# A twelve-block network: diagonals on TensorE in a state-space scan, a sum scan for a decay, keys projected behind another block, and an attention whose maxima go in threes

## The chip, the cores and the metric

The kernel runs on one core of a Trainium2 chip. The metric is the device time of one execution in microseconds (us), the median of several runs. The engines named below are PE (TensorE, matrix products, with PEld for its weight loads), DVE (VectorE), ACT (ScalarE), POOL (GpSimd) and SP (SyncE, which issues DMA transfers). PE writes its results to PSUM, from where DVE, ACT or POOL take them to SBUF.

## The reference, cut to what matters

`x` is [B=4, T=128, C=128], the context is [4, 2048, 96]. Twelve blocks are applied in turn, each as `x = x + block(layernorm(x))`: a 1-bit attention, a two-way mamba, a feed-forward layer, a 12-head attention over the context, an rwkv layer, a mixture of experts, an 8-head attention over the context, an ALiBi attention, a 1-bit feed-forward layer, a third attention over the context (the fourth layer's), a causal attention and a routed feed-forward layer. Three of them matter in detail:

```python
# mamba, once forward and once on flipped x; 256 channels d, 16 states n
def step(h, inp):
    u_t, d_t, b_t, c_t = inp
    dA = exp(d_t[:, :, None] * A)
    h = h * dA + (d_t * u_t)[:, :, None] * b_t[:, None, :]
    return h, einsum('bdn,bn->bd', h, c_t)
# rwkv: the decay of a step, and the state
w_log = -softplus(-(w0 + tanh(xw @ w1) @ w2)) - 0.5
decay = exp(-exp(w_log))          # = exp(-exp(-0.5) * sigmoid(...))
state = state * d_t + (state @ a_t) b_t + v_t k_t
# fourth layer's context attention: 8 heads of 16, keys and values from the context
q, k, v = x @ Wq + bq, y @ Wk + bk, y @ Wv + bv
out = softmax(q k^T / 4) v        # per head, over 2048 keys
return out @ Wo + bo
```

## The kernel before, in words

Everything is f32 unless said. `x` stays in SBUF as [token, batch, channel]. The blocks are methods of a class `Net` and run one after another (`program`, L2166). The code is written in a tile framework: tiles come from pools with a number of buffers, the framework adds the waits, and it may order the instructions of an engine differently from the text where nothing forbids it. Weights of the next block are fetched by `nxt()`.

Most blocks begin alike: DVE and ACT do the layer norm (`layernorm`, L343; its square root is `ln_sd`, L338, on ACT), PE turns the result over (`transposed`, L394, tiles `tr_...`), and the copy of that is the right side of the first products. While the norm runs, `busy` (L378) issues ten bf16 products on PE whose results nobody uses; they go into the tile that the transposes then overwrite. ACT's functions live in tables: when a function of another table is called, the profile shows an ACT_TABLE_LOAD of 1.28 us ahead of it.

**bit_attention** goes over units; `values` (L1112) of a unit multiplies probabilities with values into `av` and sums them (`rsum`), both from a pool of two PSUM banks (`mm`). The scores use another pool, `stp`.

**mamba** (L1238). `setup(d)` of a direction makes xd (L1285, transposes), the convolution, `xdbl`, `delta` (`softplus`, L1220, table functions Exp and Ln) and `du = delta*u` (L1344). Three bf16 parts of B and C (`x3`) are kept. The loop goes over d = 0, 1 and over n = 0 to 15. For each n, `spread` (L1349) puts row n of B (`b_ps`) and of C (`c_ps`, copied to `cs` by ACT) on all partitions with a small bf16 product; DVE makes `dbu = du*b_ps` (L1364, 128x1024); ACT makes `dA = exp(delta*A)` (L1370), in PSUM, for each half; DVE runs the recurrence for each half (L1373, `tensor_tensor_scan`, 128x512); POOL makes `hc = h*cs` (L1376); PE adds hc into `y_ps` (L1378). `setup(1)` runs in between the n of direction 0.

**grouped_ffn** (L1399): ten warming products, transposes (`tr_xnT`, L391), eight h_ps products with Gelu (L1418, L1419), y_ps products (L1425). The next block is a context attention, whose weights are first folded per group of four heads (`fold`, L473: `a_ps`, `o_ps`), from a PSUM pool of its own. Two folds are placed after h_ps 4 and 7, what is left after the block (`fold_rest`). The folds read `r_qk` and `r_vo`, which arrive by DMA. The moe block does the same for the later context attention, in expert 0 and expert 4.

**rwkv** (L1433): six mixed inputs, products through `mm` (L1457), on ACT in this order Tanh for `lo`, Square, Sigmoid for `dec` (L1502), Exp, Sigmoid for `a`, for `lg`, and Sqrt for `nrm` (L1515). The decay products within a chunk of time come from a multiplying scan `Dp`; `D = dec*Dp` and `Di = 1/D` (L1564, DVE reciprocal, 128x512) scale `al`, `be`, `kh` and `rh`, and the chunk's products follow.

**alibi, bit_ffn, narrow attention.** Behind alibi, `narrow_keys` (L679) fetches the key and value weights `w_kv` on SP and projects keys (`k_ps`, L700, copied to `kT` by ACT) and values (`v_ps`, L711, copied to `v`) of batch elements 0 and 1. Then bit_ffn runs (sums `tot` L2014, `wm`, quantized `q`, `q_tr` L2052, `h_ps` L2058). `narrow_attention` (L717) has heads in two groups s of four; one head takes 32 rows of PE. `maxima(b, s)` makes 16 products `s_ps` (L771: one head by 512 keys), each reduced to its maximum by DVE (`na_m`, L774), three PSUM banks; then `m_tr` turns the maxima over, and they are put into q. `weighted` makes transposed scores `t_ps` (L793, 32 products for four chunks of keys), Exp on ACT (`p`, L799, two of 128x1024), and 32 products into `av` (L806), these one step late. The two are woven by hand: in each of the four steps of a (b, s), two maxima, t_ps, two maxima, av; the maxima are those of the next (b, s). Batch elements 2 and 3 are projected during the steps of b = 1 and 2 with s = 0. `finish` (L816), the end of a batch element, runs in one go within the first step of the next: four copies of 17 rows by ACT and DVE in turn, `o_tr` (L822), reciprocal and multiply, `on_tr`, `oT`, `y`, add to x.

Of the kernel before, what the change touches and what calls it, by code (L numbers as in the profile page):

```python
# [18 lines left out]
P = 128  # L19
# [252 lines left out]
class Net:  # L272
# [60 lines left out]
    def root(self, v, name, eps=0, scale=1.0):  # L333

        nc = self.nc
        n = v.shape[1]
        sd = self.small(n, name + "_sd")
        nc.scalar.activation(sd, v, AF.Sqrt, bias=self.eps[:, eps : eps + 1], scale=scale)  # L338
        r = self.small(n, name + "_r")
        nc.vector.reciprocal(r, sd)  # L340
        return r

# [104 lines left out]
    def fold_open(self, es, n, heads, mask, bo):  # L447
# [11 lines left out]
        ps = raw.enter_context(self.tc.tile_pool(name=f"xr{n}_ps", bufs=2, space=PSUM))  # L459
# [6 lines left out]
        self.folds = [lambda h=h: self.fold(ps, w, h, heads, mask) for h in range(0, heads, 4)]  # L466

    def fold_rest(self):
        while self.folds:
            self.folds.pop(0)()  # L470
        self.raw.close()

    def fold(self, ps, w, h, heads, mask):  # L473
# [10 lines left out]
        mm = ps.tile([P, 512], F32, tag="xw", name="a_ps")  # L484
# [13 lines left out]
        mm = ps.tile([P, 512], F32, tag="xw", name="o_ps")  # L498
# [180 lines left out]
    def narrow_keys(self, es):  # L679

# [4 lines left out]
        self.kvp = es.enter_context(self.tc.tile_pool(name="na_kv", bufs=2))  # L685
        self.kv = {}
        with self.tc.tile_pool(name="na_kvps", bufs=3, space=PSUM) as ps:
            for b in range(2):
                for self.kv[b] in self.project(ps, b, self.nc.scalar.copy):
                    pass  # L690
# [26 lines left out]
    def narrow_attention(self, nxt):  # L717
# [9 lines left out]
        with ExitStack() as es:  # L727
# [4 lines left out]
            sp = es.enter_context(tc.tile_pool(name="na_s", bufs=3, space=PSUM))  # L732
# [3 lines left out]
            self.busy(tr, self.x, 10)  # L736
            self.layernorm(self.x, xn)
            nc.vector.tensor_add(self.x, self.x, bc_mid(self.row("bo3"), B))
# [7 lines left out]
            for s in range(2):  # L746
                nc.tensor.matmul(mm[:, s], wqo[:, s * P : s * P + P], xT, start=True, stop=True)
                nc.vector.tensor_scalar(
# [7 lines left out]
            os = []  # L756
            for j in range(2):
                t = one.tile([P, 2, P], F32, name=f"o{j}")
                nc.gpsimd.memset(t, 0.0)
                os.append(t)  # L760
            nxt()

            def maxima(b, s, kT):
# [3 lines left out]
                for j in range(4):  # L767
                    for g in range(4):
# [4 lines left out]
                        at = j * 4 + g  # L773
                        nc.vector.tensor_reduce(part[:, at : at + 1], t, axis=AX, op=ALU.max, negate=True)  # L774
                        yield
# [40 lines left out]
            def finish(b, av):  # L816
                o = os[b % 2]
                for g in range(0, P, 32):
                    self.copy(o[g : g + VW], av[g : g + VW])
# [7 lines left out]
                nc.vector.tensor_mul(on, heads[:, :, 0:ND], bc_in(r, ND))  # L827
                tr = sp.tile([P, B, P], F32, tag="s", name="on_tr")
                nc.tensor.transpose(tr[:, 0], self.flat(on), self.ident)
                oT = wk.tile([P, P], F32, tag="oT", name="oT")  # L830
                nc.scalar.copy(oT, tr[:, 0])
                y = sp.tile([P, B, P], F32, tag="s", name="y")
                nc.tensor.matmul(y[:, 0], oT, wqo[:, 2 * P : 3 * P], start=True, stop=True)
                nc.vector.tensor_add(self.x[:, b], self.x[:, b], y[:, 0])

            def run(*gens):

                gens = [iter(g) for g in gens if g is not None]
                while gens:
                    gens = [g for g in gens if next(g, gens) is not gens]  # L840
# [8 lines left out]
            take(maxima(0, 0, kv[0]), 17)  # L849
            done = None  # L850
            for b in range(B):
                av = avp.tile([P, 2, P], F32, tag="av", name="av")
                ahead = self.kv.get(b + 1)
                more = iter(()) if ahead or b + 1 == B else iter(self.project(sp, b + 1, nc.scalar.copy))
                for s in range(2):
# [5 lines left out]
                    for i in range(NCH // 4):  # L861
                        take(top, 2)
                        next(steps)
                        ahead = next(more, ahead)
                        take(top, 2)
                        next(steps)
                        if done:
                            finish(*done)
                            done = None
# [1338 lines left out]
```

## Time and profile before

| | |
|---|---|
| median of 4 runs | 1457.83 us (1454.09 to 1459.52) |
| profiled execution: own time, span | 1457.64 us, 1455.4 us |
| mean PE clock granted | 0.896 of full |
| busy: PE, DVE, ACT, POOL | 1174.9, 936.1, 644.6, 160.4 us |
| instructions | 16113 |

The blocks lie in the span about so (us): bit_attention 0 to 180, mamba to 361, grouped_ffn to 396, the 12-head context attention to 762, rwkv to 923, moe to 1004, the 8-head one to 1092, alibi to 1139, narrow_keys to 1172, bit_ffn to 1196, narrow attention to 1400, causal to 1418, routed to 1455.

In the profile's lines, `a<-b` is output and input of an operation by the program's names, L and a number the line in the kernel, x and a number how many there are. Numbers are us, or ns where a group's mean is meant. In timeline lines, what stands in brackets is the engine's idle time before the operation and what ended it. One matrix product in f32 shows as two records on PE.

### The profile page before, as it was taken

What the parts mean: (1) busy time and instruction counts of PE and PEld (TensorE: products, weight loads), DVE (VectorE), ACT (ScalarE), POOL (GpSimd) and SP (SyncE); (2) the same over time, 40 slices, a digit from 0 to 9 for tenths busy, and PEclk for the clock granted to TensorE, in tenths of its full rate; (3) what the DMA queues carried; (4) which work ended last, traced back from release to release, by engine and by line L of the source; (5) the groups of instructions that cost most, each with busy time, mean ns of one, the idle gap of its engine ahead of it and who ended that gap; (6) DMA issues with size and microseconds to landing.
All of it is one profiled execution on the core that took longest, in us unless ns stands there. A gap on an engine that the chain in (4) does not pass through costs nothing.

```text
span 1455.4 us, 16113 instructions
## 1 busy us (share of the span) xinstructions
PE 1174.9 (81%) x6362; PEld 620.9 (43%) x6373; DVE 936.1 (64%) x1632; ACT 644.6 (44%) x865; POOL 160.4 (11%) x153
## 2 busy tenths in 40 slices
PE   2477557676899999999996735899979748999978
PEld 0156322223644444444433314575444434565644
DVE  8987678897257667766765797513667365544635
ACT  3732255443356555655654210233645531444432
POOL 0036105365000000000000120000004000000000
PEclk9788668799999999999999976999999866999989
DMA  6000000000600000000001000510000000000010
GB/s 180 0 1 2 0 1 0 29 1 18 183 0 0 0 0 0 1 0 0 1 0 58 1 0 1 144 27 22 0 2 2 10 6 1 2 2 2 2 55 8
DMA packets 9486, 27.84 MB, mean 19 GB/s; under 512 B 1191, under 2 KB 7120, under 8 KB 8350
## 3 DMA queue, kind: packets, MB, share of 16 engines
q1 hardware_dynamic: 8286, 24.88, 6.0%
q10 hardware_dynamic: 1120, 1.88, 0.4%
q8 instruction: 52, 0.85, 0.2%
q14 instruction: 28, 0.23, 0.0%
HBM read 26.49 MB, written 0.26 MB: 18 GB/s over the span
## 4 chain that ended last, share of the span: by engine, by line
PE 63%; DVE 17%; ACT 5%; issue 4%; POOL 1%; DMA 1%; another core or an unknown queue 0%; DVEq 0%; ACTq 0%; SPq 0%; POOLq 0%
PE av L615 14%; PE sc L581 13%; PE s_ps L771 5%; DVE h L1373 3%; PE t_ps L793 2%; PE k_ps L700 2%; PE h_ps L1801 2%; PE y_ps L1813 2%; PE mm L1457 2%; PE y_ps L1378 2%; PE av L806 1%; POOL hc L1376 1%; PE q_ps L533 1%; DVE dbu L1364 1%; PE v_ps L711 1%
## 5 line engine op out<-in xcount | busy, mean ns | idle before, releaser
L615 PE MATMUL av<-s,ctx 128*97 128x512 f32 x448 | 208.0, 600 | 6.5 <-ACT s L613 6.4
L581 PE MATMUL sc<-q_aug,ctxT 99*128 99x512 f32 x448 | 209.1, 593 | 0.0
L612 DVE TENSOR_TENSOR s<-s,mbs 128x1024 f32<-128x1024 f32 x112 | 132.3, 1217 | 38.8 <-ACT mbs L607 38.8
L583 ACT COPY s<-sc 128x1024 f32<-128x1024 f32 x112 | 113.0, 1009 | 96.6 <-PE sc L581 96.3
L613 ACT ACTIVATE s<-s 128x1024 f32<-128x1024 f32 x112 | 115.4, 1056 | 35.6 <-DVE s L612 35.0
L591 DVE TENSOR_TENSOR m<-m,s 128x1024 f32<-128x1024 f32 x72 | 87.9, 1221 | 65.0 <-ACT s L583 65.0
L774 DVE TENSOR_REDUCE na_m<-s_ps 128x1 f32<-128x512 f32 x128 | 83.0, 686 | 69.4 <-PE s_ps L771 69.1
L615 PEld LDWEIGHTS av<-s,ctx 128*97 128x97 f32 x448 | 73.5, 166 | 125.7 <-issue 105.0
L581 PEld LDWEIGHTS sc<-q_aug,ctxT 99*128 99x128 f32 x448 | 81.0, 189 | 88.0 <-issue 77.8
L1378 PE MATMUL y_ps<-hc,consts 128*128 128x512 f32 x128 | 76.2, 729 | 29.3 <-POOL hc L1376 27.8
L799 ACT ACTIVATE p<-t_ps 128x1024 f32<-128x1024 f32 x64 | 62.4, 1021 | 63.7 <-PE t_ps L793 62.0
L771 PE MATMUL s_ps<-kT,q 32*128 32x512 f32 x256 | 84.5, 710 | 1.7 <-DVE na_m L774 1.7
L1376 POOL TENSOR_TENSOR hc<-h,cs 128x1024 f32<-128x1024 f32 x32 | 75.8, 2380 | 85.6 <-DVE h L1373 85.5
L1373 DVE TENSOR_TENSOR_SCAN h<-dA,dbu 128x512 f32<-128x512 f32 x64 | 74.1, 1201 | 4.1 <-ACT dA L1370 4.0
L1378 PEld LDWEIGHTS y_ps<-hc,consts 128*128 128x128 f32 x128 | 26.4, 226 | 82.4 <-POOL hc L1376 56.5
L793 PE MATMUL t_ps<-q,kT 32*128 32x128 f32 x1024 | 55.6, 297 | 1.6 <-ACT p L799 1.6
L1370 ACT ACTIVATE dA<-delta,A 128x508 f32<-128x508 f32 x64 | 42.8, 687 | 29.4 <-DVE h L1373 29.2
L793 PEld LDWEIGHTS t_ps<-q,kT 32*128 32x128 f32 x1024 | 45.9, 195 | 14.6 <-issue 9.4
L382 PEld LDWEIGHTS <-consts 128*128 128x128 bf16 x169 | 18.7, 120 | 69.3 <-issue 54.9
L1479 POOL TENSOR_SCALAR pick_r<-consts,cols 128x16 f32<-128x16 f32 x1 | 0.5, 484 | 408.2 <-PE av L615 408.2
L1817 DVE SCALAR_TENSOR_TENSOR x<-y_ps,cw,x 128x128 f32<-128x128 f32 x32 | 9.0, 343 | 48.0 <-PE y_ps L1813 44.1
L700 PE MATMUL k_ps<-ctxT,w_kv 97*128 97x512 f32 x64 | 34.6, 685 | 5.8 <-DMA w_kv<-in_kv 5.8
(603 smaller groups left out, 2015.8 us busy)
## 6 DMA issues: line engine op xcount, KB each, us to landing
w_moe<-in_moe SPq DMA_DIRECT2D x2, 2048.0 KB, 8.6
ctxT<-in_ctxT SPq DMA_DIRECT2D x3, 768.0 KB
w_l3f<-in_l3f SPq DMA_DIRECT2D x1, 1920.0 KB, 7.6
rows<-in_rows ACTq DMA_DIRECT2D x1, 1664.0 KB, 12.7
w_l0f<-in_l0f SPq DMA_DIRECT2D x1, 1024.0 KB
w_mamba<-in_mamba SPq DMA_DIRECT2D x1, 976.0 KB, 18.6
w_r<-in_r SPq DMA_DIRECT2D x1, 960.0 KB
consts<-in_consts SPq DMA_DIRECT2D x1, 832.0 KB, 16.8
```

What stands on the lines that cost most here:

```text
L581: nc.tensor.matmul(sc[:, i], self.ctxT[:, at : at + P], u.q, start=True, stop=True)
L583: nc.scalar.copy(s, sc)
L591: nc.vector.tensor_max(u.m, u.m, u.s[j])
L612: nc.vector.tensor_sub(p, p, bc_mid(u.mb, 2))
L613: nc.scalar.activation(p, p, AF.Exp)
L615: nc.tensor.matmul(u.av[: DC + 1], self.ctx[:, u.b * NCH + chunks[2 * j + i]], p[:, i], start=j + i == 0, stop=j == n - 1 and i == 1)
L771: nc.tensor.matmul(t, qs[rows], kT[rows, s, j * 512 : j * 512 + 512], start=True, stop=True)
L774: nc.vector.tensor_reduce(part[:, at : at + 1], t, axis=AX, op=ALU.max, negate=True)
L793: nc.tensor.matmul(ts[g // 2][:, g % 2, j], kT[g * 32 : g * 32 + 32, s, at : at + P], qs[g * 32 : g * 32 + 32], start=True, stop=True)
L1373: nc.vector.tensor_tensor_scan(h[:, half], self.flat(dA), dbu[:, half], 0.0, ALU.mult, ALU.add)
L1376: nc.gpsimd.tensor_mul(hc, h, bc_mid(cs, 2))
L1378: nc.tensor.matmul(y[:, half], self.ident, hc[:, half], start=n == 0, stop=n == 15)
```

## The change

It is one bundle of edits, block by block:

- bit_attention: the last unit's `av` and `rsum` take banks of the scores' pool.
- mamba: ten warming products become seven, and ten each are added before `xdbl` and the first transposes of du; the Ln table is called for ahead of its use; dA moves from PSUM to SBUF; for three of four n, `dbu` is no longer made by DVE but by PE, as du transposed (`duT`) times a diagonal matrix of B's row (`dg`, four ACT activations each), into PSUM (`dbu_ps`, three banks); `hc` has two buffers in place of three.
- folds use the running block's own PSUM tiles; moe's first fold moves behind the block.
- rwkv: the decay is summed by a scan before the exponential, and two Exps give D and Di; the ACT functions are re-ordered so that fewer tables change; six warming products in place of ten in its second half.
- `table` calls for a table ahead of its use (grouped_ffn, moe, narrow attention); `zero_after` makes a zero that depends on a tile, to hold an order.
- narrow_keys runs behind bit_ffn; only the DMA of its weights stays where it was (`narrow_open`).
- narrow attention: maxima in groups of 3, 2, 3, 2, 3, 2, 1, products of a group ahead of its reduces; `finish` in four parts spread over the steps, with one copy in place of four; seven warming products in place of ten; both q products ahead of their DVE work.
- causal and routed: six warming products in place of ten.

```diff
+    def table(self, func, last):
+        self.nc.scalar.activation(self.small(1, "table"), last, func, bias=self.eps[:, 0:1], scale=0.0)
+    def zero_after(self, x, name):
+        z = self.small(1, name)
+        self.nc.vector.tensor_scalar(z, x, 0.0, 0.0, ALU.max, ALU.min)
+        return z
...
-        self.folds = [lambda h=h: self.fold(ps, w, h, heads, mask) for h in range(0, heads, 4)]
-    def fold_rest(self):
+        self.folds = [lambda ps, h=h: self.fold(ps, w, h, heads, mask) for h in range(0, heads, 4)]
+    def fold_rest(self, ps):
         while self.folds:
-            self.folds.pop(0)()
-        self.raw.close()
+            self.folds.pop(0)(ps)
...
-    def narrow_keys(self, es):
+    def narrow_open(self, es):
         pool = es.enter_context(self.tc.tile_pool(name="na_w", bufs=1))
         self.wkv = pool.tile(list(self.A["kv3"].shape), F32, name="w_kv3")
         self.nc.sync.dma_start(self.wkv, self.A["kv3"])
         self.kvp = es.enter_context(self.tc.tile_pool(name="na_kv", bufs=2))
+        self.nps = es.enter_context(self.tc.tile_pool(name="na_s", bufs=3, space=PSUM))
+    def narrow_keys(self):
         self.kv = {}
-        with self.tc.tile_pool(name="na_kvps", bufs=3, space=PSUM) as ps:
-            for b in range(2):
-                for self.kv[b] in self.project(ps, b, self.nc.scalar.copy):
-                    pass
+        for b in range(2):
+            for self.kv[b] in self.project(self.nps, b, self.nc.scalar.copy):
+                pass
...
-            self.busy(tr, self.x, 10)
+            self.busy(tr, self.x, 7)
             self.layernorm(self.x, xn)
+            self.table(AF.Exp, self.sd[:, 0:1])
...
+                at = 0
+                for n in (3, 2, 3, 2, 3, 2, 1):
+                    several = []
+                    for at in range(at, at + n):
+                        j, g = divmod(at, 4)
                         t = sp.tile([P, 512], F32, tag="s", name="s_ps")
                         rows = slice(g * 32, g * 32 + 32)
                         nc.tensor.matmul(
                             t, qs[rows], kT[rows, s, j * 512 : j * 512 + 512], start=True, stop=True)
-                        at = j * 4 + g
+                        several.append((at, t))
+                    for at, t in several:
                         nc.vector.tensor_reduce(part[:, at : at + 1], t, axis=AX, op=ALU.max, negate=True)
-                        yield
+                    at += 1
+                    yield
...
             def finish(b, av):
-                o = os[b % 2]
-                for g in range(0, P, 32):
-                    self.copy(o[g : g + VW], av[g : g + VW])
+                o = wk.tile([P, 2, P], F32, tag="o", name="o")
+                nc.scalar.copy(o, av)
+                yield
                 tr = sp.tile([P, B, P], F32, tag="s", name="o_tr")
                 for s in range(2):
                     nc.tensor.transpose(tr[:, s], o[:, s], self.ident)
@@ -825,20 +839,16 @@
                 nc.vector.reciprocal(r, heads[:, :, ND])
                 on = wk.tile([P, NH, ND], F32, tag="on", name="on")
                 nc.vector.tensor_mul(on, heads[:, :, 0:ND], bc_in(r, ND))
+                yield
                 tr = sp.tile([P, B, P], F32, tag="s", name="on_tr")
                 nc.tensor.transpose(tr[:, 0], self.flat(on), self.ident)
                 oT = wk.tile([P, P], F32, tag="oT", name="oT")
                 nc.scalar.copy(oT, tr[:, 0])
+                yield
                 y = sp.tile([P, B, P], F32, tag="s", name="y")
                 nc.tensor.matmul(y[:, 0], oT, wqo[:, 2 * P : 3 * P], start=True, stop=True)
                 nc.vector.tensor_add(self.x[:, b], self.x[:, b], y[:, 0])
...
-                        take(top, 2)
+                        take(top, 1)
                         next(steps)
+                        take(fin, 1)
                         ahead = next(more, ahead)
-                        take(top, 2)
+                        take(top, 1)
                         next(steps)
                         if done:
-                            finish(*done)
-                            done = None
+                            fin, done = finish(*done), None
+                        take(fin, 1)
                         ahead = next(more, ahead)
                         if s == 0:
...
+                        if u is units[-1]:
+                            return stp.tile([P, W], F32, tag="st", name=name)
+                        return ps.tile([P, 512], F32, tag="mm", name=name)
...
+        if first:
+            self.table(AF.Ln, e[:, 0, 0:1])
...
-                t = das.tile([P, B, T], F32, name=f"dA{j}")
-                nc.vector.memset(t[:, :, 0:1], 0.0)
+                t = one.tile([P, B, T], F32, name=f"dA{j}")
+                nc.gpsimd.memset(t[:, :, 0:1], 0.0)
...
+                duT = wk.tile([P, 2, B, P], F32, tag="duT", name="duT")
+                for half in range(2):
+                    nc.vector.tensor_mul(du[:, half], delta[:, half], u[:, half])
+                    tr = mm_tile("du_tr").rearrange("p (b t) -> p b t", b=B)
+                    if d == 0 and half == 0:
+                        self.busy(tr, e[:, 0].rearrange("p (b t) -> p b t", b=B), 10)
+                    for b in range(B):
+                        nc.tensor.transpose(tr[:, b], du[:, half, b * T : b * T + T], self.ident)
+                    nc.scalar.copy(duT[:, half], tr)
+                yield u, zs, x3, bt, delta, du, duT
...
-                    bn = spread(x3, n, "b_ps")
                     cn = spread(x3, 16 + n, "c_ps")
                     cs = lp.tile([P, N], F32, tag="cs", name="cs")
                     nc.scalar.copy(cs, cn)
-                    dbu = lp.tile([P, 2, N], F32, tag="dbu", name="dbu")
-                    nc.vector.tensor_mul(dbu, du, bc_mid(bn, 2))
+                    if n % 4 == 3:
+                        t = lp.tile([P, 2, N], F32, tag="dbu", name="dbu", bufs=2)
+                        nc.vector.tensor_mul(t, du, bc_mid(spread(x3, n, "b_ps"), 2))
+                        dbu = [t[:, half] for half in range(2)]
+                    else:
+                        dg = lp.tile([P, B, T], F32, tag="dg", name="dg")
+                        for b in range(B):
+                            nc.scalar.activation(dg[:, b], self.ident, AF.Copy, scale=bt[:, b, n : n + 1])
+                        dbu = []
+                        for half in range(2):
+                            t = dps.tile([P, N], F32, tag="dbu", name="dbu_ps")
+                            for b in range(B):
+                                nc.tensor.matmul(
+                                    t[:, b * T : b * T + T], duT[:, half, b], dg[:, b], start=True, stop=True)
+                            dbu.append(t)
...
-                            h[:, half], self.flat(dA), dbu[:, half], 0.0, ALU.mult, ALU.add)
-                    hc = lp.tile([P, 2, N], F32, tag="hc", name="hc")
+                            h[:, half], self.flat(dA), dbu[half], 0.0, ALU.mult, ALU.add)
+                    hc = lp.tile([P, 2, N], F32, tag="hc", name="hc", bufs=2)
...
+            self.table(AF.Sqrt, hT[:, 7, 0:1])
...
+                cum = tmp("cum", pool=ta)
+                nc.vector.tensor_tensor_scan(cum, self.flat(keep), dec, 0.0, ALU.mult, ALU.add)
+                z = self.zero_after(lg[:, 0:1], "rw_z1")
                 nc.vector.tensor_scalar(nkk, k, self.col("k_k"), -1.0, ALU.mult, ALU.mult)
-                nc.vector.tensor_mul(nkk, nkk, self.flat(m))
+                nc.vector.tensor_mul(nkk, nkk, self.flat(rl))
+                nc.scalar.activation(
+                    D[:, :, 1:], cum.rearrange("p (c t) -> p c t", t=CH), AF.Exp, bias=z,
+                    scale=-math.exp(-0.5))
+                nc.scalar.activation(Di, cum, AF.Exp, bias=z, scale=math.exp(-0.5))
...
-                Dp = tmp("Dp", pool=tb)
-                nc.vector.tensor_tensor_scan(Dp, self.flat(ds), self.flat(start), 0.0, ALU.mult, ALU.add)
-                al = nkk
-                nc.vector.tensor_mul(al, nkk, Dp)
-                D = dec
-                nc.vector.tensor_mul(D, dec, Dp)
-                Di = tmp("Di", tag="start", pool=tb)
-                nc.vector.reciprocal(Di, D)
...
+                nc.vector.tensor_mul(chunked(al), chunked(nkk), D[:, :, 0:CH])
                 nc.vector.tensor_mul(be, kb, Di)
                 nc.vector.tensor_mul(kh, k, Di)
-                nc.gpsimd.tensor_mul(rh, r, D)
+                nc.gpsimd.tensor_mul(chunked(rh), chunked(r), D[:, :, 1:])
...
-                fT, df = mixing(xn, "ln_ffn_w", "ln_ffn_b", tc_, ((xp, 10),))
+                fT, df = mixing(xn, "ln_ffn_w", "ln_ffn_b", tc_, ((xp, 6),))
...
+                if e == 7:
+                    self.table(AF.Sqrt, hT[:, 3, 0:1])
...
-            qT, kT, mm = self.queries_keys_values(w, ("b3_q", "b3_k"), one, wk, ps)
+            qT, kT, mm = self.queries_keys_values(w, ("b3_q", "b3_k"), one, wk, ps, 6)
...
-                net.narrow_keys(nes)
+                net.narrow_open(nes)
+            if BLOCKS[i][0] == "bit_ffn":
+                net.narrow_keys()
...
```

## The prediction

> **What bounds the kernel now.** The blocks run one after another, and which engine limits changes from block to block, so I read the page first, then busy time by stage, the chain that ended last, and the timeline wherever the diff touches. All durations are of the profiled execution: its span is 1455.4 us, its own time 1457.64 us, 2.2 us outside the span, and the median of four runs is 1457.83 us, so nothing has to be rescaled. A difference of 0.3%, 4.4 us, is about what a measurement of this kernel can tell from no change.
>
> ```profile
> PEclk9788668799999999999999976999999866999989
> PE 63%; DVE 17%; ACT 5%; issue 4%; POOL 1%; DMA 1%; another core or an unknown queue 0%; DVEq 0%; ACTq 0%; SPq 0%; POOLq 0%
> L774 DVE TENSOR_REDUCE na_m<-s_ps 128x1 f32<-128x512 f32 x128 | 83.0, 686 | 69.4 <-PE s_ps L771 69.1
> L1378 PE MATMUL y_ps<-hc,consts 128*128 128x512 f32 x128 | 76.2, 729 | 29.3 <-POOL hc L1376 27.8
> L1373 DVE TENSOR_TENSOR_SCAN h<-dA,dbu 128x512 f32<-128x512 f32 x64 | 74.1, 1201 | 4.1 <-ACT dA L1370 4.0
> ```
>
> TensorE carries 63% of the chain, VectorE 17%. The biggest PE groups (L615, L581, the 12-head context attention) are not touched. What is touched lies in slices where the clock row falls to 6 or 8, and in the last attention.
>
> The busy table by window (us, PE with count, PEld, DVE, ACT, POOL, clock) says which engine limits:
>
> ```profile
> 180.00:212.70 32.70, 18.70 (x40) 6.12 (x40) 22.87 (x44) 17.50 (x23) 0.38 (x4) 0.66 0.00 1
> 212.70:289.00 76.30, 53.08 (x102) 19.89 (x102) 66.47 (x64) 40.42 (x59) 32.17 (x14) 0.78 0.04 14
> 289.00:357.10 68.10, 49.12 (x112) 17.80 (x112) 63.38 (x58) 30.21 (x50) 43.66 (x19) 0.95 0.00 0
> 1172.00:1206.00 34.00, 13.55 (x65) 6.90 (x66) 27.60 (x68) 7.13 (x10) 0.85 (x4) 0.65 0.02 7
> 1206.00:1400.00 194.00, 179.98 (x2426) 111.08 (x2424) 94.96 (x171) 82.94 (x106) 0.00 (x0) 0.91 0.01 2
> ```
>
> Mamba's loop (second and third line) is DVE's: 87% and 93%. bit_ffn (fourth) waits in a DVE chain at a cold clock. The narrow attention (last) is PE's, 93%. The chain of waits, start and length, shows three pure losses:
>
> ```profile
> 360.81 9.74 DMA r_vo<-in_vo
> 803.94 3.36 DVE Di L1564
> 1138.76 7.92 DMA w_kv<-in_kv
> ```
>
> **Part by part** (minus is time saved).
>
> *bit_attention's end.* The last unit's av (158.13, 3.61 us) waits for a `mm` bank of the unit before it, its probabilities being ready by 155.2; in the score pool's banks it starts about 2.5 us sooner. −2.5 (0 if that bank is late too, to −3).
>
> *Mamba's setup.* Three of ten warming matmuls of 0.41 go but xn is ready at 183.97, so only 0.9 of them was waited for; the Ln table's 1.28 is loaded ahead; the cold 3.78 us of the dt matmuls shorten by half. Added on the path: four small matmuls and a copy, then du's half (0.69), transposes, a 0.59 copy and eight matmuls in place of one dbu multiply. First scan 212.69 → 210.3: −2.4 (0 to −5).
>
> *Mamba's loop.* This is a steady stretch of direction 1, 6.72 us for two n:
>
> ```profile
> 317.61 4.55 DVE L1373 TENSOR_TENSOR_SCAN h<-dA,dbu 128x512 f32<-128x512 f32 x4
> 322.08 2.32 DVE L1364 TENSOR_TENSOR dbu<-du,b_ps 128x1024 f32<-128x1024 f32 x2
> 324.32 4.55 DVE L1373 TENSOR_TENSOR_SCAN h<-dA,dbu 128x512 f32<-128x512 f32 x4
> ```
>
> DVE goes scan, dbu, scan with nothing between: 3.36 per n. For three n in four dbu leaves DVE, which then needs (8×1.14+1.17)/4 = 2.6 per n. PE's share grows: 1.72 for y, 0.22 for c, 0.05 for b (one in four), and 24 matmuls of 128 columns in four n, which as two-pass f32 cost 0.22 to 0.235 by the nearest row (out_ps), so 5.3 to 5.6 per four: 3.4 per n. ACT, with twelve 0.2 to 0.27 us diagonals, comes to 2.6, POOL keeps 2.34. dA moves from PSUM to SBUF; no row shows a scan fed the new way, and I take Exp and scan at their old 0.65 and 1.14. PE becomes the limit. Direction 1 is then a draw (16×3.4+7 us of fill against 61). Direction 0, first scan to first scan, takes 83 us, because setup(1)'s DVE and ACT work shares it; DVE drops by 12×1.17=14, PE needs 54 plus 9.9 of setup(1), 64. Of the 14 I take 6, as the PSUM→PE→PSUM chain must fit three dbu banks. −6 (+8, if PE's order adds half a us per n in direction 1, to −18).
>
> *grouped_ffn.* The first fold waits for a DMA, and the transposes stand behind it on PE:
>
> ```profile
> 370.60 0.33 PE L489 MATMUL a_ps<-r_vo,r_qk 64*99 64x1 f32 x2 [3.67 <-DMA r_vo<-in_vo]
> 371.17 0.66 PE L391 MATMUL tr_xnT<-consts,xn 128*128 128x128 f32 x4
> ```
>
> xn is ready at 366.9. The folds now draw on the block's own `mm` tiles, and in the built order they follow the transposes: 371.17−366.9=4.3, plus 1.7 of fold matmuls between xnT's copy (ending 372.5) and h_ps at 374.21. −6 (−5 to −7). The fold still has its 11 us before w_vo is needed.
>
> *rwkv's projections.* Five table loads of 1.28 stand between 782.0 and 792.2; two remain on this path, −3.8. The decay runs as a sum scan and two Exps, so Di's reciprocal (3.36) and the D product (0.69) leave DVE ahead of al, be and kh, −4.0; the scan (1.23, as Dp's) now lies under ACT's work, −1.2. A Sqrt load is added before rw_sd, under a DVE multiply and sum of 1.4; without that cover it costs 1.3. −9 (−5 if ACT's loads were hidden under DVE, −12).
>
> *Warming matmuls 10→6* in rwkv's ffn, causal and routed: each series ends 1.2 us after its xn (the transposes 914.70 against xn 913.42, likewise 1403.38 against 1401.95 and 1420.08 against 1418.83). 3×−1.2=−3.6 (+2 each if the shorter series leaves four more passes cold, as dt's four at 0.9 are where warm ones take 0.43). The windows above show the clock already down to 0.66 and 0.65 around such starts. The Trainium skill, "TensorE: Matmul & The Clock Gate", Part 1, speaks against the cut: full clock comes only after a busy stretch of about 3.4 us, so six of them might not open it. By an estimate from that rule the slower start of each block would eat what the series saves, and the sum below would be 3.6 smaller. My sum goes by the row: the transposes wait for the series.
>
> *moe.* The fold moves between experts on an engine that is 98% busy (0); the Sqrt load at 999.92, 1.28, comes forward. −1.2 (0 to −3).
>
> *narrow_keys behind bit_ffn.* Today keys and values of two batch elements wait for w_kv (issued 1138.76, PE idle 5.83), then hold PE to 1171.5, and bit_ffn's sums queue behind them:
>
> ```profile
> 1146.82 10.42 PE L700 MATMUL k_ps<-ctxT,w_kv 97*128 97x512 f32 x16 [5.83 <-DMA w_kv<-in_kv]
> 1172.05 0.38 PE L2014 MATMUL tot<-bf_s,ones 128*128 128x2 f32 x2 [0.53 <-ACT v L714]
> 1172.47 0.16 DVE L2016 TENSOR_SCALAR wm<-tot 128x2 f32<-128x2 f32 x1 [13.62 <-PE tot L2014]
> ```
>
> DVE had idled 13.62 us, so tot could run at 1158.9. From tot to the next block's transposes (1196.78) is 24.7 us with PE mostly free, and the built order sets k and v matmuls into it (w_kv's DMA keeps its place on SP). 1158.9+24.7=1183.6, plus 2 us for ln_sd behind three 0.59 kT copies on ACT and matmuls behind k's: 1185.6, −11 (−13 to −4, when ACT's 34 copies of about 0.5, 17 us, come ahead of bit_ffn's).
>
> *Narrow attention, end of a batch element.* Ordinary steps take 3.95 us (s_ps at 1347.01, then 1350.96). The step with `finish` is 1363.48 to 1371.47, 8.0:
>
> ```profile
> 1364.86 0.43 DVE L328 COPY o<-av 17x256 f32<-17x256 f32 x1 [0.43 <-ACT o L326]
> 1365.35 0.44 PE L822 MATMUL o_tr<-consts,o 128*128 128x128 f32 x2 [0.94 <-DVE o L328]
> 1370.47 1.07 PE L806 MATMUL av<-p,v 128*17 128x128 f32 x32
> ```
>
> Four alternating copies, then PE waits for each link. Spread over steps with one copy, PE adds only o_tr, on_tr and y, 1.3: 8.0−3.95−1.3=−2.8, three times; the last one saves three copies, −1.4. −9.8 (−5 if links still arrive late).
>
> *Maxima in threes.* A pair takes 0.96 on PE (row groups overlap), a three about the same, but the pair behind it needs the second of the three's 0.65 us reduces, with three banks: +0.6. Three steps of 3+2 maxima at 4.55 and one of 3.45 are 17.1 against 16.2 (1343.06 to 1359.27): +0.9 in five stages, +0.5 in two that also project keys: +5.5 (−7 without a stall, +6). The trace's reduces (0.686 mean) bound it; the Trainium skill, "TensorEngine Tiling (Array Packing)", Performance Considerations, says likewise that tiling quickens TensorE but not the emptying of PSUM, and its up to fourfold gain for contractions of 32 rows, taken alone, would make a three free on PE. By that gain the sum below would be 12.5 larger. I stay with the banks' count.
>
> *Its start:* Exp load ahead −1.0, three warming matmuls fewer −1.0, both q matmuls before their DVE work −0.5: −2.5 (0 to −3). The new av memset (0.28) hides under PE.
>
> Sum: −2.5−2.4−6−6−9−3.6−1.2−11−9.8+5.5−2.5=−48.5; 1457.6−48.5=1409.1, say 1409.
>
> **Rivals.** (1) Mamba gains nothing because PE, now at 3.4 per n of the old 3.36, is the limit: for it, the count; against, direction 0's DVE load. Loop +8 in place of −6: 1423. (2) Threes stall, finish links arrive late, and ACT's copies delay bit_ffn: narrow's loop +1 in place of −4.3, keys −4 in place of −11: 1421. (3) Slower than before: in mamba the ring scan (2.3), hc (2.36), y (1.72), dbu (1.8), 8.2 us for one n, does not overlap enough through two hc and three dbu banks. Today's 144 us are 4.5 per n; all else saves 42.5, so it decides from 4.5+42.5/32=5.8 per n; at 6.2 it is 1469. Against: two n in flight give 4.1. (4) Fewer stalls than I count, with mamba at −18 and threes free: 1385.
>
> **Numbers.** Forecast (1396 to 1420) 0.58, rival 1 0.15, rival 2 0.15, rival 3 0.05, rival 4 0.05, and 0.02 for rivals 1 and 2 together with the shortened warming series costing all three places, within 0.3%. So faster 0.93, same 0.02, slower 0.05. The range 1386 to 1434 takes in the forecast, rivals 1 and 2 and their sum in part.
>
> **What would show it.** First scan near 210; direction 1 with PE full and DVE at three quarters; h_ps of grouped_ffn near 368; products near 797 in a time base shifted by the gains before; no DVE wait of 13 us before tot; steps of 4.5 us in the narrow attention with no 8 us step. It is wrong if mamba's scans wait on dbu_ps with PE idle, or if the last attention's steps exceed 5 us.

## The result, and the profile after

The change leaves the time where it was: 1458.81 us (median of 44 runs) against 1457.45 us (69 runs), ratio 1.0016 with a 95% interval of 1.0004 to 1.0027. The forecast was 1409 us. The profiled execution of after has a span of 1454.4 us, before 1455.4 us. These lines of the page answer to those shown of before:

```profile
PEclk9688789889889999999999996699999987999999
PE 58%; DVE 9%; ACT 3%; issue 2%; DMA 1%; POOL 0%; DVEq 0%; ACTq 0%; SPq 0%
L786 DVE TENSOR_REDUCE na_m<-s_ps 128x1 f32<-128x512 f32 x128 | 82.4, 685 | 62.6 <-PE s_ps L782 62.1
L1437 PE MATMUL y_ps<-hc,consts 128*128 128x512 f32 x128 | 80.3, 768 | 43.0 <-POOL hc L1435 42.8
L1432 DVE TENSOR_TENSOR_SCAN h<-dA,dbu_ps 128x512 f32<-128x512 f32 x48 | 56.2, 1206 | 48.2 <-PE dbu_ps L1421 42.5
```

The last two lines hold the answer. All 64 scans had stood still for 4.1 us before; the 48 that take the new products of PE now stand still for 48.2 us, of which 42.5 are ended by `dbu_ps`. And PE itself stands 43.0 us ahead of y, waiting for POOL's hc (29.3 before). The chain's shares add up to 73% only: it could be followed back no further than to a y product at 400.29 us, so it says nothing of mamba, and the windows have to.

I cut both traces at the same events (first or last instruction of a block on its engine) and compare lengths in us:

| stretch | before | after | difference | forecast |
|---|---|---|---|---|
| start to xd (bit_attention) | 180.5 | 175.0 | −5.5 | −2.5 |
| xd to mamba's first scan | 32.2 | 32.4 | +0.2 | −2.4 |
| first scan to grouped_ffn | 151.4 | 206.2 | **+54.8** | **−6** |
| grouped_ffn | 33.0 | 26.6 | −6.4 | −6 |
| 12-head context attention | 371.6 | 370.3 | −1.3 | 0 |
| rwkv to its chunk products | 39.5 | 30.4 | −9.1 | −9 |
| rwkv's rest | 118.8 | 115.7 | −3.1 | −1.2 |
| moe | 72.2 | 76.5 | +4.3 | −1.2 |
| 8-head context attention | 92.1 | 92.4 | +0.3 | 0 |
| alibi to the narrow attention's q | 110.6 | 93.6 | −17.0 | −11 |
| narrow attention, from q | 197.9 | 182.3 | −15.6 | −6.8 |
| causal and routed | 55.6 | 53.0 | −2.6 | −2.4 |

Eleven stretches together lose 56 us in these two traces, more than the 42.5 forecast; mamba's loop gives it all back. This is one trace of each kernel. In the traces of the experiments below, five rows differ from kernel to kernel although their code is the same as in after: bit_attention takes 175.0 to 177.8 us, rwkv to its chunk products 28.6 to 33.7, alibi to q 93.5 to 96.8, the narrow attention 182.3 to 188.3, causal and routed 52.9 to 58.2. The after column has the low end of four of the five, so 56 us is a favourable reading. grouped_ffn (26.5 to 26.6) and moe (76.4 to 77.0) are steady.

The windows of the two directions of mamba's loop (columns as in the prediction) show no engine full:

```profile
207.40:316.20 108.80, 82.48 (x320) 48.59 (x319) 64.35 (x61) 61.16 (x116) 39.69 (x16) 0.86 0.03 10
316.20:397.80 81.60, 59.64 (x265) 36.13 (x263) 45.11 (x40) 38.28 (x80) 35.00 (x15) 0.94 0.00 1
```

In direction 1 PE is busy for 73%, DVE for 55%. Before, DVE alone had been full there, 55.36 of 55.6 us:

```profile
297.00:352.60 55.60, 41.22 (x96) 15.23 (x96) 55.36 (x51) 26.40 (x43) 35.45 (x16) 0.94 0.00 0
```

The timeline of a stretch of direction 1 after the change shows who waits for whom:

```profile
361.56 1.98 PE L1437 MATMUL y_ps<-hc,consts 128*128 128x512 f32 x4 [0.33 <-POOL hc L1435]
363.38 2.39 PE L1421 MATMUL dbu_ps<-dg,duT 128*128 128x128 f32 x20
...
364.09 3.44 DVE L1432 TENSOR_TENSOR_SCAN h<-dA,dbu_ps 128x512 f32<-128x512 f32 x3 [4.09 <-PE dbu_ps L1421]
...
365.45 4.66 POOL L1435 TENSOR_TENSOR hc<-h,cs 128x1024 f32<-128x1024 f32 x2 [3.95 <-DVE h L1432]
...
367.86 5.40 PE L1437 MATMUL y_ps<-hc,consts 128*128 128x512 f32 x8 [1.87 <-POOL hc L1435]
...
373.09 0.38 PE L1396 MATMUL b_ps<-x,sel 96*128 96x512 bf16 x1
...
373.51 1.22 DVE L1411 TENSOR_TENSOR dbu<-du,b_ps 128x1024 f32<-128x1024 f32 x1 [5.98 <-PE b_ps L1396]
```

Read it as a circle. The scans end at 367.5 and nothing is prepared for DVE. PE's queue has y of two states next; it stands for hc, which POOL made from those scans, then runs y until 373.09 (5.40 us for eight passes, partly at half clock: 0.51 was granted from 370.1 to 371.5). Only then come b_ps and dbu_ps of the next states, for which DVE has waited 6 us. One state costs 5.1 us (20.5 for four, by the scans' starts) where it cost 3.36.

### The profile page after: what moved, and what is told of

It reads as the page before. It is cut to its first block, busy times and chain, and to the rows that moved or that the text cites. A ratio compares the mean times of both kernels' runs of the same rounds, so it can differ in the third digit from the quotient of the medians.

```text
span 1454.4 us, 17011 instructions
## 1 busy us (share of the span) xinstructions
PE 1204.1 (83%) x6755; PEld 669.5 (46%) x6767; DVE 906.3 (62%) x1603; ACT 672.9 (46%) x966; POOL 161.6 (11%) x154
## 4 chain that ended last, share of the span: by engine, by line
PE 58%; DVE 9%; ACT 3%; issue 2%; DMA 1%; POOL 0%; DVEq 0%; ACTq 0%; SPq 0%
PE av L624 13%; PE sc L590 13%; PE s_ps L782 5%; PE t_ps L806 2%; PE mm L1518 2%; PE h_ps L1867 2%; PE y_ps L1879 2%; PE av L819 2%; PE k_ps L711 2%; PE q_ps L542 1%; DVE qa L1742 1%; PE y L635 1%; PE v_ps L722 1%; DVE pt L1749 1%; PE sc L1982 1%
## 5 line engine op out<-in xcount | busy, mean ns | idle before, releaser
L1437 PE MATMUL y_ps<-hc,consts 128*128 128x512 f32 x128 | 80.3, 768 | 43.0 <-POOL hc L1435 42.8
L1432 DVE TENSOR_TENSOR_SCAN h<-dA,dbu_ps 128x512 f32<-128x512 f32 x48 | 56.2, 1206 | 48.2 <-PE dbu_ps L1421 42.5
L1421 PEld LDWEIGHTS dbu_ps<-dg,duT 128*128 128x128 f32 x384 | 51.2, 202 | 19.5 <-issue 9.5
L1421 PE MATMUL dbu_ps<-dg,duT 128*128 128x128 f32 x384 | 52.0, 286 | 6.8 <-DVE h L1432 6.8
```

The lines of the kernel that those rows point to most:

```text
L1421: nc.tensor.matmul(t[:, b * T : b * T + T], duT[:, half, b], dg[:, b], start=True, stop=True)
L1437: nc.tensor.matmul(y[:, half], self.ident, hc[:, half], start=n == 0, stop=n == 15)
```

## The experiments

**Mamba taken out, and mamba alone.** The first run puts `mamba` and `softplus` of before into the changed kernel; the second puts those of the change into the kernel before.

> The changed kernel with the mamba block and softplus of before; all other parts of the change stay. From the two traces mamba's loop grew from 151.4 to 206.2 us and everything else lost 56 us. Theory A (all of the loss is made inside mamba's loop and what is gained elsewhere is independent of it): 1403 us, 1398 to 1409, ratio to before 0.963. Rival (the other blocks are faster in the trace only because of what mamba leaves behind, such as weights that have landed meanwhile or a PE that is warm): half or more of the 56 us vanishes, 1425 to 1457 us.

> The kernel of before with only the changed mamba block and softplus. Theory A: the loop costs 54.8 us more and setup nothing, 1457.5+55=1512 us, 1505 to 1518. Rival (the loss depends on the other parts): 1465 to 1495 us.

Measured: 1412.5 us, ratio 0.9703 (0.9673 to 0.9732), and 1508.6 us, ratio 1.0391 (1.0364 to 1.0419). Mamba's loop takes 150.0 us in the first kernel and 206.3 in the second. So the loss is made in mamba's loop, and it does not depend on the rest. 1412.5 us lies above the 1398 to 1409 expected: the ratio is worth 43 us, not 56. The missing 13 us are not mamba's. The trace of this kernel has the other blocks 16 us longer than after's, in five rows whose code is the same: bit_attention 177.6 us, rwkv's projections 33.6, alibi to q 95.8, narrow attention 188.3, causal and routed 55.1. The 43 us come close to the 42.5 that the forecast had for everything but the loop, but single parts were off by up to 9 us to one side and 5 to the other, so it is in part luck that this sum came out.

**The order on PE.** The y products of a state are issued after the dbu products and scans of the next, nothing else:

```diff
-                    for half in range(2):
-                        nc.tensor.matmul(y[:, half], self.ident, hc[:, half], start=n == 0, stop=n == 15)
+                    def add(n=n, hc=hc):
+                        for half in range(2):
+                            nc.tensor.matmul(y[:, half], self.ident, hc[:, half], start=n == 0, stop=n == 15)
+                    adds.append(add)
+                    if len(adds) > 1:
+                        adds.pop(0)()
```

> The changed kernel; in mamba's loop the y products of n are issued after the dbu products, Exps and scans of n+1 instead of at the end of n. No work is added or removed, banks and buffers stay. Theory A (PE takes its queue in order: dbu products that the scans need stand behind y products that wait for POOL's hc of 2.4 us): the scans no longer wait for the pair hc and y, a state costs 3.5 to 4.2 us instead of 5.1 in direction 1, and the time falls by 25 to 50 us to 1409 to 1434. Rival B (the added work itself is the cost: 0.39 us diagonals on ACT and 5.5 us of PE products per four states): stays within 10 us of 1458.8. Rival C (three dbu banks are the limit): stays within 15 us, since the banks are the same.

Measured: 1435.5 us, ratio 0.9877 (0.9848 to 0.9906): 23 us back, direction 1 at 4.3 us a state, both just outside theory A's ranges. In the trace the loop takes 178.1 us in place of 206.2. The edit changes the order and nothing else, so the order is what these 28 us were lost to; the rest is still there.

**Four banks for dbu** (`mb_dbu` 3→4, `mb_ps` 3→2):

> The changed kernel with four dbu banks in PSUM instead of three, and two instead of three for mamba's other products. Rival C (three banks, one and a half states, force a serial chain): two whole states fit, 30 us or more come back, below 1430. Theory A: the order of PE's queue is still made with y ahead of dbu in places, so a part comes back, 5 to 25 us, 1434 to 1454, and the scans still wait for dbu products behind y. Rival B (the work is the cost): within 5 us of 1458.8, or slower, since two banks for setup's products are fewer.

Measured: 1464.6 us, ratio 1.0067 (1.0045 to 1.0089): nothing comes back. Direction 1 takes 84.2 us against 81.6, direction 0 104.6 against 108.8. A fourth bank, which is the risk that the forecast had named, does not free the loop as long as y stands where it does. Mamba's other products lost a bank in the same edit, so the fourth bank was not tried quite alone. Rival B had this number right, though its reason falls with the runs on the order; theory A's 5 to 25 us did not come.

**One state late with three hc buffers, and two states late** (`> 1` above becomes `> 2`; hc has three buffers and the dbu tile on SBUF one in both):

> As the run with y products one state late (1435.5 us, direction 1 at 4.3 us a state), and hc gets three buffers instead of two, for which dbu on SBUF gets one instead of two. Theory A (the rest of the loss is also waiting: PE's queue stands at y for POOL's hc, hc for a buffer that y frees): 3.6 to 4.0 us a state, 1415 to 1428 us. Rival B (from here on the work itself is the cost, ACT's diagonals among it): within 5 us of 1435.

> As before, but the y products of n come two states late, after the dbu products of n+2, with three hc buffers. Theory A: PE never stands at y for POOL, what remains is PE's work of 3.4 us a state, or POOL's and ACT's chain; 3.4 to 3.7 us a state in direction 1, 1405 to 1425 us, and not below the kernel with the old mamba block by more than 8 us. Rival B: within 5 us of 1435.

Measured: 1437.0 us (0.9870, 0.9832 to 0.9908) and 1409.4 us (0.9678, 0.9646 to 0.9709). With y one state late a third hc buffer is worth nothing (the loop takes 178.1 us with it and without it), against theory A; the second state of delay is worth 27 us more, and the loop takes 153.0 us. The third buffer belongs to that second state: three hc are then alive at once. The windows of the latter kernel's two directions:

```profile
207.00:294.00 87.00, 71.73 (x318) 45.55 (x318) 70.35 (x61) 62.50 (x118) 39.73 (x16) 0.91 0.04 13
294.00:347.00 53.00, 51.85 (x265) 33.85 (x263) 44.80 (x39) 38.30 (x80) 35.52 (x15) 1.00 0.00 1
```

PE is now busy for 98% of direction 1, at full clock, 3.3 us a state: the count of 3.4 in the forecast holds once the queue is in an order that lets it. In its timeline PE goes dbu, y, dbu, y without a wait:

```profile
321.65 1.95 PE L1422 MATMUL dbu_ps<-dg,duT 128*128 128x128 f32 x16
...
323.43 1.88 PE L1439 MATMUL y_ps<-hc,consts 128*128 128x512 f32 x4
...
325.37 1.95 PE L1422 MATMUL dbu_ps<-dg,duT 128*128 128x128 f32 x16
...
327.16 1.88 PE L1439 MATMUL y_ps<-hc,consts 128*128 128x512 f32 x4
```

This kernel is 3.2% faster than before. No run is clearly faster; the old mamba block in the changed kernel, with or without late y (1410.9 and 1412.5 us), can't be told from it.

**Late y in the old loop.** The same delay of two states, in the changed kernel with the old mamba block:

> The changed kernel with the old mamba block (1412.5 us), and in this old loop the y products two states late. Theory A (the order of PE's queue matters only once the scans wait for products of PE in f32 that stand behind y; in the old loop DVE is the limit and b_ps runs ahead): direction 1 stays at 55 to 56 us, the whole within 3 us of 1412.5. Rival (late y products are worth something by themselves): direction 1 below 52 us, 8 us or more off.

Measured: 1410.9 us (0.9659, 0.9589 to 0.9729), direction 1 at 55.6 us as without the delay. The old loop has nothing to gain from the order: b_ps, the only product its DVE waits for, costs PE 0.22 us and runs ahead. So with PE's order mended the new loop (153.0 us to grouped_ffn: directions 87.2 and 52.7, end 13.2) and the old one (82.9, 55.6, 11.5, or 150.0) are equal within what the runs tell apart. Moving dbu to PE gains nothing here even then.

**Every second state on DVE** (`n % 4 == 3` becomes `n % 2 == 1`, y two states late), once with moe's fold behind expert 0:

> The changed kernel with y products two states late (1409.4 us) and every second state's dbu on DVE instead of every fourth. Counted work a state: DVE 2.28+1.17/2=2.87, PE 1.72+0.22+0.11+0.92=2.97, ACT 2.5. Theory A (with PE's order mended, the busiest engine's count holds, as 3.4 for PE did: direction 1 took 52.7 us): 3.0 a state, direction 1 46 to 49 us, the whole 1398 to 1405 us. Rival (POOL's hc chain, 2.36 and a wait, holds a state at 3.3): 1407 to 1411 us.

> As the run with every second dbu on DVE and late y, and moe's fold issued behind expert 0 instead of expert 4. The moe block took 72.2 us before and 76.5 in every run with the change. Theory A (the fold had filled PE's wait of 1.75 us for b_ps and kept it at full clock for the first products): moe 72 to 74 us, 2.5 to 4.5 us off the whole. Rival (the first products are slow for another reason, the weights' arrival or the block's start): moe stays at 76 to 77.

Measured: 1421.4 us (0.9733, 0.9663 to 0.9804) and 1421.2 us (0.9720, 0.9643 to 0.9797). The first run missed both of its expectations; in the second theory A fell and the rival was right. Direction 1 became slower (57.0 us), at 3.5 us a state where the busiest engine counts 2.97. The first kernel's timeline shows where:

```profile
319.55 4.67 POOL L1436 TENSOR_TENSOR hc<-h,cs 128x1024 f32<-128x1024 f32 x2 [2.34 <-DVE h L1433]
...
322.88 3.54 DVE L1433 TENSOR_TENSOR_SCAN h<-dA,dbu 128x512 f32<-128x512 f32 x2
...
326.34 2.30 DVE L1433 TENSOR_TENSOR_SCAN h<-dA,dbu_ps 128x512 f32<-128x512 f32 x2
```

Two scans that take dbu from PSUM last 2.30 us, two that take it from SBUF 3.54: the first of these alone 2.43 us. It starts at 322.88, POOL's hc ends at 324.22, and the scan ends 1.1 us later, about one scan's length, as if it had stood until POOL was done. The trace has more of it: of the 32 scans whose dbu lies in SBUF, the 13 that run beside an hc take 2352 ns in the mean, the other 19 take 1199; scans that take dbu from PSUM take 1188 beside an hc. moe stayed at 77.0 us.

**Where dA lies.** Two runs put every state's dbu on DVE (`if n >= 0`), one with dA in SBUF as in the change, one with dA in the three PSUM banks that the dbu products had used.

> The changed kernel with every state's dbu on DVE, so that PE has no dbu products in the loop; dA stays in SBUF. Theory A (a scan that reads dA and dbu both from SBUF does not start or go on while POOL's hc runs): after each pair of scans hc takes 2.36 us, only the dbu multiply (which reads one side from PSUM) can run beside it, so a state costs about 2.4+2.3=4.7 us, direction 1 74 to 80 us, the whole 1445 to 1460 us. Rival (scans run at 1.19 us wherever dA lies, and the long ones had another reason): direction 1 55 to 57 us, 1408 to 1418 us.

> The same with dA in three PSUM banks again (those that dbu products had). Both theories: direction 1 55 to 57 us, 1410 to 1418 us; what differs from the other run is the place of dA alone.

Measured: 1453.4 us (0.9974, 0.9951 to 0.9998) and 1417.7 us (0.9727, 0.9688 to 0.9766). 36 us for the place of one operand (and one memset by POOL instead of DVE). The scan group of the first kernel and of the second:

```profile
L1432 DVE TENSOR_TENSOR_SCAN h<-dA,dbu 128x512 f32<-128x512 f32 x64 | 103.5, 1664 | 0.9
```

```profile
L1432 DVE TENSOR_TENSOR_SCAN h<-dA,dbu 128x512 f32<-128x512 f32 x64 | 73.8, 1203 | 1.6 <-ACT dA L1429 1.3
```

DVE does not stand idle ahead of its scans; the scans are longer. In the first kernel the 33 scans that run beside an hc take 2096 ns in the mean, the 31 others 1203. In the second, with dA in PSUM, the 35 beside an hc take 1203 as well. POOL suffers too: in direction 1 six of the sixteen hc take 3.08 to 3.12 us in the first kernel, and none over 2.37 in the second. Direction 1 took 75.6 us against 56.4, within theory A's 74 to 80. So it takes both: two operands in SBUF, and POOL at work. The Trainium skill, "SBUF — State Buffer", "SBUF: two separate sides", states the rule behind it: a DVE operation with two SBUF inputs and a GpSimd operation that reads SBUF take turns on a port pair, and the one that comes second waits until the first is done. The runs agree.

**The narrow attention.** In the changed kernel with the old mamba block (1412.5 us), maxima in twos, and the end of a batch element in one go:

```diff
-                for n in (3, 2, 3, 2, 3, 2, 1):
+                for n in (2,) * 8:
```

> The changed kernel with the old mamba block (1412.5 us) and maxima in twos instead of 3,2,3,2,3,2,1; the spread end of a batch element stays. The trace of the changed kernel shows steps of 4.55 us with threes against 3.95 before, as the prediction had it. Theory A (threes cost +0.9 in five stages and +0.5 in two, since the second pair waits for the reduces of the three): 1407 us, 5.5 less than 1412.5. Rival (the three's cost is won back in the fourth step, which holds one maximum in place of four): 1411 to 1415 us. Other side (threes gain): 1417 or more.

> The changed kernel with the old mamba block (1412.5 us), and the end of a batch element in one go again, with its single copy. Theory A (PE waits at each link of the end's chain, 2.8 us three times, less the three copies that stay away, 1.2 each): 4 to 8 us more, 1416 to 1421. Rival (the chain was hidden by the framework's own order): within 2 us of 1412.5.

Measured: 1419.5 us (0.9716, 0.9656 to 0.9776) and 1417.7 us (0.9731, 0.9694 to 0.9767), against 0.9703 (0.9673 to 0.9732): neither can be told from it by the time. The stages, from m_tr to m_tr, can be read. A stage without projection took 16.5 us before, 17.0 to 17.4 in threes, 16.5 again in twos; a stage with projection 33.8 and 32.1 before, 28.9 with the change, 29.1 in twos, 30.5 with the end in one go. So threes cost 0.5 to 0.9 in a stage without projection and nothing in one with it. The end's spreading gains 1.3 to 1.6 a time; the rest of the 3 to 5 us is there already with the end in one go. One copy in place of four differs there, and so do the groups of products; which of the two it is was not tried. The steps of threes are as forecast, 4.55 us:

```profile
1352.76 0.72 PE L782 MATMUL s_ps<-kT,q 32*128 32x512 f32 x3
...
1357.31 0.70 PE L782 MATMUL s_ps<-kT,q 32*128 32x512 f32 x3
```

**Keys first again** (`narrow_keys` called right behind alibi, in the changed kernel with the old mamba block):

> The changed kernel with the old mamba block (1412.5 us), and the keys and values projected ahead of bit_ffn again. Theory A (bit_ffn's sums queue behind them on PE): from alibi's start to narrow attention's q products 110 us in place of 95.7, 1424 to 1428 us. Rival (the start of the narrow attention then gains from a PE that is warm, or bit_ffn was slowed by ACT's copies as much): 1412 to 1418 us.

Measured: 1418.2 us (0.9729, 0.9642 to 0.9816), between the two expectations; by the whole time it can't be told from the other order. From alibi to q it takes 105.4 us, where the traces with keys behind bit_ffn have 93.5 to 96.8: in this stretch the order is worth 9 to 12 us. The other 5 us by which 105.4 lies below before's 110.6 belong to other edits, which were not taken apart.

## Why the prediction was wrong

**The step that failed** is mamba's loop, and in it the sentence that PE becomes the limit at 3.4 us a state and that 6 of the 14 us stay. It counted busy time engine by engine and took for granted that PE can do its work in any order. PE takes its queue in order, and the built kernel has y products, which wait for POOL's hc, ahead of dbu products, which the next scans wait for. Before, only a cheap b_ps stood on that path. Now scan (2.3), hc (2.36), y (1.72) and dbu form a circle. With y two states later in the queue, and none of the loop's work taken away, 3.3 us a state were measured and 49 of the 55 us came back (1458.8 to 1409.4; in the traces the loop goes from 206.2 to 153.0). The −6 did not come even then: 153.0 stands against 151.4 before, which is the draw that rival 1 had. I had the circle as rival 3, at 6.2 us a state over 4.5, +54 us, which is what the loop cost; its chance of 0.05 was the error. Its reason, too few buffers, was not the one: a fourth dbu bank, or a third hc buffer with y one state late, gave nothing back. Its 1469 us did not come because the other blocks lost more than the 42.5 us forecast.

**A term that was not priced**: dA's move to SBUF, which I took at no cost for want of a row. It lengthens only scans whose dbu lies in SBUF too, sixteen of 64 in the change (1484 ns mean against 1206), about 4.5 us of DVE time (16 times 278 ns); with all 64 it makes some 36 us. ACT's diagonals cost 0.39 us each (four of them 1.26), not 0.2 to 0.27, without becoming the limit. Two readings were off without weight: direction 0 took 84.3 us before, not 83, and keys and values of two batch elements are 28 copies, not 34.

**What held.** grouped_ffn −6.4 (−6), the step in threes 4.55 (4.55), the keys' order 9 to 12 (11), and rwkv −9.1 (−9) in this trace, −5.8 to −10.9 over the traces of the same code. In grouped_ffn the transposes no longer stand behind the fold:

```profile
415.88 1.02 PE L402 MATMUL tr_xnT<-consts,xn 128*128 128x128 f32 x4
417.68 4.56 PE L1477 MATMUL h_ps<-xnT,w_l0f 128*128 128x512 f32 x10 [0.79 <-DVE xnT L328]
...
422.47 0.25 PE L498 MATMUL a_ps<-r_vo,r_qk 64*99 64x1 f32 x2
```

In rwkv Di is an Exp of 0.71 us in place of a 3.36 us reciprocal:

```profile
838.41 0.71 ACT L1598 ACTIVATE Di<-cum,rw_z 128x512 f32<-128x512 f32 x1
```

And bit_ffn's sums wait no longer; k_ps waits for its weights behind them:

```profile
1175.12 0.16 DVE L2085 TENSOR_SCALAR wm<-tot 128x2 f32<-128x2 f32 x1 [0.42 <-PE tot L2083]
...
1179.15 7.74 PE L711 MATMUL k_ps<-ctxT,w_kv 97*128 97x512 f32 x12 [4.14 <-DMA w_kv<-in_kv]
```

The end of a batch element is taken apart as forecast: one copy, and av at its usual distance.

```profile
1368.79 1.07 PE L819 MATMUL av<-p,v 128*17 128x128 f32 x32
1369.92 0.37 ACT L832 COPY o<-av 128x256 f32<-128x256 f32 x1 [0.61 <-PE av L819]
...
1371.78 0.41 PE L836 MATMUL o_tr<-consts,o 128*128 128x128 f32 x2
...
1373.93 1.07 PE L819 MATMUL av<-p,v 128*17 128x128 f32 x32
```

**What was off in size.** bit_attention's end −5.5 for −2.5 (−2.7 in the slowest trace of the same code), setup +0.2 for −2.4, moe +4.3 for −1.2. In moe the trace shows where: the first eight h_ps of before and of after are

```profile
933.44 3.68 PE L1801 MATMUL h_ps<-xT,w_moe 128*128 128x512 f32 x8
963.86 6.14 PE L1867 MATMUL h_ps<-xT,w_moe 128*128 128x512 f32 x8
```

The granted clock of the block's first 10 us is 0.77 in place of 1.00, and the first y_ps comes 13.2 us after the block's start in place of 10.0. All traces with the changed rwkv and moe have these slow first products (5.0 to 6.5 us), and the kernel in which mamba alone was changed has not (3.68). Which of the edits lowers the clock there was not tried, so the cause stays open; the shorter warming series in rwkv's ffn is one of them. Nor is any gain shown for the warming products that were saved in causal and routed: 52.9 to 58.2 us stand against 55.6 before.

Of the narrow attention's −15.6, 6.6 are its first stage, 23.5 us before and 16.9 after. I don't credit these to the change: the traces of kernels with the very same code for it show 16.8 to 20.7 us, and with maxima in twos 26.7, as the clock happens to rise early or late.

## What to carry to other kernels

When work moves to another engine, count its busy time, but then read the order of its queue: an engine is full only if nothing that waits for a third engine stands ahead of what the first one needs next. Let the consumer of a slow result (here y behind POOL) come one or two rounds later in the queue, and give the loop the buffers that this order needs; buffers without the order gave nothing here. And when an operand of a DVE operation moves from PSUM to SBUF, look whether its other operand lies there too and POOL is at work.

## What the runs showed of the hardware that I had not expected

DVE's scans and POOL's products get in each other's way once a scan reads both operands from SBUF: 1203 ns mean against 1664, and beside an hc 1203 against 2096.

PE can be busy and yet stay at half clock. In the kernel with maxima in twos, windows of the narrow attention's first stages (PE's busy time after the length, the clock third from the end) read:

```profile
1195.00:1205.00 10.00, 9.52 (x81) 5.09 (x80) 3.87 (x6) 3.00 (x4) 0.00 (x0) 0.50 0.01 2
1205.00:1215.00 10.00, 10.00 (x114) 5.77 (x113) 3.91 (x7) 2.74 (x3) 0.00 (x0) 0.54 0.01 2
```

20 us of nearly unbroken work, most of it products of 32 rows, left the clock near 0.50. The rows agree with the clock: 32 av products take 1.91 us at 1201.44 and 1.07 at 1214.86. The Trainium skill, "TensorE: Matmul & The Clock Gate", Part 1, has it rise after a busy window of about 3.4 us; here it did not, and the measurement decides. Why it stays low is open. It makes this stage differ by several us from run to run, so effects of under 6 us are read from other stages here and not from whole times.
